# A graph layer's last stage: the output blocks take every fourth node instead of 128 neighbours

## The chip, the cores and the metric

One core of a Trainium2 chip runs the whole kernel in one launch. The metric is the device time in microseconds (us) of one execution. Engines are named as in the profile: PE (TensorE, with PEld for its weight loads), DVE (VectorE), ACT (ScalarE), POOL (GpSimd), SP (SyncE, which here only issues DMAs).

## The reference, cut to what matters

12500 nodes of 128 features, 212500 edges sorted by destination, 8 attention heads of 16. The first part sums messages along the edges into `h`. The change is in what comes after it: a batch norm over all nodes, a residual, and a layer norm over the features of each node.

```python
h = x + h_attn
mean = h.mean(axis=0)
var = jnp.mean((h - mean) ** 2, axis=0)
y = (h - mean) * jax.lax.rsqrt(var + BN_EPS) * bn_gamma + bn_beta
out = _layernorm(x + y, axis=-1)     # (v - mean) / sqrt(var + 1e-5), per node
```

## The kernel before, in words

Most of the time goes to the edges: 208 groups of up to eight tiles of 128 edges, for which rows are gathered, scored and summed into `hx`. `hx` holds `h` transposed, one feature per partition and one node per column. None of that is changed. Near its end the loop is written out by hand (L814 to L878), and batch norm statistics are gathered on the way; `norm_scale` (L407) closes them into a scale `ab[:, 0]` per feature.

The last stage (`last_stage`, L889) then works through the nodes in 25 chunks of 512 columns (`B4`); the last has 212 (`width`, L455). The transposed input `x` lies beside it, loaded as `XR[i]` in the same layout (L464).

For each chunk TensorE makes a PSUM bank `ps` of 128 x 4 x 128: up to 128 nodes on the partitions, four blocks, 128 features. A matmul takes 128 columns of `XR`, `hx` or `Y` as its stationary weights and streams the matrix `cent` (or `scaled_cent`, which carries the batch norm's scale), which subtracts the mean over the features; so the result is turned back to one node per partition and centred at once. Each fp32 matmul appears as two passes in the profile, so four blocks are eight. There are three ways to fill a bank (`centred`, L925):

- Chunks in `AHEAD` (0 to 6, 12, 18) add `x` through `part_of_x` (L746 to L748) and `hx` through L934. For chunks 0 to 6 the part from `x` runs before the statistics are closed (`ahead`, L752).
- Chunks 7, 8 and 9 get scale and residual on VectorE (L908), the rest on GpSimd (L910, L911), into a tile `Y`; L945 then multiplies `Y`.
- L937 or L940 adds the batch norm's shift to those chunks that do not have it.

Then, for each pair of chunks: ScalarE squares the bank and sums, either with one whole square and a reduce on VectorE (L960, L961) or block by block with an accumulator (L965); one root per pair (L967); VectorE takes the reciprocal (L971) and scales the bank into the SBUF tile `o` (L977, L982); a DMA writes `o` to the output (L979, L983). The pairs are (0), (1), (2,3), ... (22,23), (24). The order on the engines is the order of the code (L988 to L998): residual of a pair, centring and variance of the pair two before it, scaling of the pair three before it. Every output DMA is issued from SP, but that of chunk 23 and of chunk 24's partial block from ACT, behind ACT's own work in program order.

In the kernel before, `blocks` (L742) cuts a chunk into runs of 128 neighbouring columns. So partition p of block k holds node 128k + p of the chunk, and a partition's four rows of 512 B lie 64 KB apart in the output. Chunk 24 has a block of 128 and one of 84, and each has a scale and a DMA of its own.

Of the kernel before, what the change touches and what calls it, by code (L numbers as in the profile page):

```python
# [13 lines left out]
OP = mybir.AluOpType  # L14
# [3 lines left out]
P = 128  # L18
# [21 lines left out]
def plan(N, T):  # L40

    n, r = divmod(T - sum(LAST), U)
    sizes = [U] * n + [r] * (r > 0) + list(LAST)
    assert n > 1 and len(sizes) % 2 == 0
    starts = [sum(sizes[:g]) for g in range(len(sizes))]
    cuts = list(range(0, N - 64, CH)) + [N - 64, N]
    due = {}
    thr = [0.0] * len(sizes)
    for j, c in enumerate(cuts[1:]):
        need = (c + (64 if c < N - CH else 24)) * T  # L50
        g = next((g for g, t in enumerate(starts) if t * N >= need), None)
        if g is not None:
            due.setdefault(g, []).append(j)
            thr[g] = float(c)
    return sizes, starts, cuts, due, thr
# [27 lines left out]
def gnn_kernel(  # L83
# [19 lines left out]
    nc = tc.nc  # L103
# [3 lines left out]
    usizes, ustarts, cuts, due, _ = plan(N, T)  # L107
# [39 lines left out]
    hx = consts.tile([P, N + P], F32, name="hx")  # L147
# [47 lines left out]
    cent = consts.tile([P, P], F32, name="cent")  # L195
# [218 lines left out]
    def norm_shift():  # L414
        nc.vector.tensor_mul(ab[:, 1:2], ab[:, 0:1], mv[:, 0:1])
        nc.vector.tensor_sub(ab[:, 1:2], gb[:, 1:2], ab[:, 1:2])
# [33 lines left out]
    B4 = 4 * P  # L450
    NY = -(-N // B4)
    XR = {}
    todo = list(range(NY))

    def width(i):  # L455
        return min(B4, N - i * B4)
# [238 lines left out]
    for q in range(NQ):  # L695
# [3 lines left out]
        for g, a in piece.get(q, []):  # L699
            if a == 0:  # L700
                i = free.pop(0)
# [5 lines left out]
        k = q - first_step  # L707
# [32 lines left out]
    RING = ["ps_e", "ps_e", "ps_q", "ps_q", "ps_t", "ps_t", "ps_a", "ps_m"]  # L740

    def blocks(i):  # L742
        n = width(i)
        return [(k, min(P, n - k * P)) for k in range(-(-n // P))]

    def part_of_x(i, ps):  # L746
        for k, m in blocks(i):
            nc.tensor.matmul(ps[:m, k, :], XR[i][:, k * P:k * P + m], cent, start=(k == 0), stop=False)  # L748

    PX = {}  # L750

    def ahead(i):  # L752
        if i in AHEAD:
            r = RING[i % len(RING)]
            PX[i] = psp.tile([P, 4, P], F32, name=r, bufs=RING.count(r))
            part_of_x(i, PX[i])
# [132 lines left out]
    def last_stage(fin, bank, PX):  # L889
        Y, PY, V = {}, {}, {}  # L890


        pick = fin.tile([P, P], BF16, name="pick", bufs=1)
        nc.gpsimd.memset(pick, 0.0)
        for r in (0, 32, 64):
            nc.gpsimd.memset(pick[r:r + 1], 1.0)
        shift = fin.tile([P, P], BF16, name="shift", bufs=1)
        scaled_cent = fin.tile([P, P], F32, name="scaled_cent", bufs=1)

        def residual(i):  # L900

            c, n = i * B4, width(i)
            if i in AHEAD:
                return
            Y[i] = fin.tile([P, B4], F32, name="y", bufs=8)
            y, h = Y[i][:, :n], hx[:, c:c + n]
            if i in on_vector:
                nc.vector.scalar_tensor_tensor(y, h, ab[:, 0:1], XR[i][:, :n], op0=OP.mult, op1=OP.add)  # L908
            else:
                nc.gpsimd.tensor_scalar(y, h, ab[:, 0:1], ab[:, 1:2], op0=OP.mult, op1=OP.add)  # L910
                nc.gpsimd.tensor_tensor(y, y, XR[i][:, :n], op=OP.add)  # L911

        def split_shift():
            ps = bank(7)[:65, 0, :]
            nc.tensor.matmul(ps, ab[:, 1:2].to_broadcast([P, 65]), cent, start=True, stop=True)
            rest = fin.tile([P, P], F32, name="rest", bufs=1)
            mid = fin.tile([P, P], BF16, name="mid", bufs=1)
            nc.scalar.activation(shift[:65], ps, AF.Copy)
            nc.vector.tensor_sub(rest[:65], ps, shift[:65])
            residual(8)  # L920
            nc.scalar.activation(mid[:65], rest[:65], AF.Copy)
            nc.scalar.activation(shift[32:33], mid[32:33], AF.Copy)
            nc.vector.tensor_sub(shift[64:65], rest[64:65], mid[64:65])

        def centred(i):  # L925
            PY[i] = ps = PX[i] if i in PX else bank(i)
            c, full = i * B4, i in AHEAD
            if i == 0:
                split_shift()
            if full:  # L930
                if i not in PX:
                    part_of_x(i, ps)
                for k, m in blocks(i):
                    nc.tensor.matmul(ps[:m, k, :], hx[:, c + k * P:c + k * P + m], scaled_cent, start=False,  # L934
                                     stop=False)
            if i < 2:
                nc.tensor.matmul(ps, ab[:, 1:2].to_broadcast([P, P]), cent[:, None, :].to_broadcast([P, 4, P]),  # L937
                                 start=False, stop=True)
            elif full or i in on_vector:
                nc.tensor.matmul(ps, pick[:65], shift[:65, None, :].to_broadcast([65, 4, P]), start=not full,  # L940
                                 stop=full)
            if not full:
                whole = i in on_vector
                for k, m in blocks(i):
                    nc.tensor.matmul(ps[:m, k, :], Y[i][:, k * P:k * P + m], cent, start=not whole,  # L945
                                     stop=(k == 3 or not whole))

        def spread(p):
            nb = len(blocks(p[-1]))
            return V[p[0]][:, :len(p), :nb, 0]  # L950

        def variance(p):
            v = fin.tile([P, 2, 4, 1], F32, name="v", bufs=4)
            V[p[0]] = v
            if blocks(p[-1])[-1][1] < P:
                nc.vector.memset(v, 1.0)
            for h, i in sorted(enumerate(p), key=lambda e: e[1] not in by_reduce):
                if i in by_reduce:
                    sq4 = fin.tile([P, 4, P], F32, name="sq4", bufs=2)
                    nc.scalar.activation(sq4, PY[i], AF.Square, scale=P ** -0.5)  # L960
                    nc.vector.tensor_reduce(v[:, h, :, 0], sq4, axis=AX.X, op=OP.add)  # L961
                else:
                    sq = fin.tile([P, P], F32, name="sq")
                    for k, m in blocks(i):
                        nc.scalar.activation(sq[:m], PY[i][:m, k, :], AF.Square, scale=P ** -0.5,  # L965
                                             accum_out=v[:m, h, k, :])
            nc.scalar.activation(spread(p), spread(p), AF.Sqrt, bias=eps)  # L967

        def scaled(p):
            v = V[p[0]]  # L970
            nc.vector.reciprocal(spread(p), spread(p))  # L971
            o = fin.tile([P, 2, 4, P], F32, name="o")
            for h, i in enumerate(p):
                bl = blocks(i)
                c, fb = i * B4, sum(m == P for _, m in bl)
                if fb:
                    nc.vector.tensor_tensor(o[:, h, :fb, :], PY[i][:, :fb, :],  # L977
                                            v[:, h, :fb, :].to_broadcast([P, fb, P]), op=OP.mult)
                    (nc.scalar if i == NY - 2 else nc.sync).dma_start(  # L979
                        out[c:c + fb * P, :].rearrange("(c p) d -> p c d", p=P), o[:, h, :fb, :])  # L980
                for k, m in bl[fb:]:
                    nc.vector.tensor_scalar(o[:m, h, k, :], PY[i][:m, k, :], v[:m, h, k, :], None, op0=OP.mult)  # L982
                    nc.scalar.dma_start(out[c + k * P:c + k * P + m, :], o[:m, h, k, :])  # L983

        nc.vector.tensor_scalar(scaled_cent, cent, ab[:, 0:1], None, op0=OP.mult)
        norm_shift()
        residual(7)
        for i in range(len(pairs) + 5):  # L988
            for f, k in ((residual, i), (centred, i - 2), (variance, i - 2), (scaled, i - 3)):
                if 0 <= k < len(pairs):  # L990
                    if f in (residual, centred):
                        for c in pairs[k]:
                            if c not in Y or f == centred:
                                f(c)
                    else:
                        f(pairs[k])
                    if f == scaled and k == 0:
                        residual(9)  # L998
# [144 lines left out]
```

## Time and profile before

| | |
|---|---|
| three runs | 2698.18, 2701.23 (median), 2709.0 us |
| the profiled execution | 2704.18 us, its span 2702.4 us, 37686 instructions |
| busy share of the span | PE 71%, DVE 61%, POOL 58%, PEld 42%, ACT 24% |
| statistics closed, last stage begins | about 2662 us |
| last matmul pass of the stage ends | 2690.6 us |
| last scale ends, last output DMA issued | 2695.9 us |
| output DMAs | 23 of 256 KB and one of 64 KB from SP, one of 256 KB and one of 42 KB from ACT |

Times inside the execution count from the start of its span. Shares over the whole span say little about this change, since the stage is 40 of 2702 us: it has to be read in stretches and by its own lines. A busy PE in the table means passes in flight, which overlap.

### The profile page before, as it was taken

The numbers are of one execution on the slowest core, as the hardware profiler recorded it, in microseconds if no ns is written. First come the engines' busy times: TensorE is split into PE (matmuls) and PEld (weight loads), VectorE is DVE, ScalarE is ACT, GpSimd is POOL, SyncE is SP. The second block draws the span as 40 slices with busy tenths as digits, with TensorE's granted clock in tenths as the row PEclk, the third lists the DMA queues.
The fourth block names the chain that finished last, engine by engine and source line by source line (L and its number), as shares of the span: only waits on it lengthen the run. The fifth ranks groups of instructions, "written<-read, shape, count | busy, mean of one in ns | idle before, by whom it ended". The sixth has DMA issues, their size and how long they took to land. (4 is left out here: it accounts for less than half of the span.)

```text
span 2702.4 us, 37686 instructions
## 1 busy us (share of the span) xinstructions
PE 1926.2 (71%) x9414; PEld 1144.2 (42%) x9414; DVE 1644.1 (61%) x3598; ACT 658.4 (24%) x2477; POOL 1579.8 (58%) x1673
## 2 busy tenths in 40 slices
PE   7787766767777767667675767667777767677677
PEld 5454433433434434334333444334344434444446
DVE  3456665565666565666554665656656656656577
ACT  2242222222222222222221222222222222222225
POOL 5645665565666666565654666665656665656624
PEclk8888888887888878888777888878778887878899
DMA  7744444444454444454444544444544444544454
GB/s 225 237 138 139 139 133 143 127 145 135 136 144 141 135 140 141 129 151 130 141 139 117 145 134 135 139 140 130 146 134 140 141 141 132 149 133 140 141 174 127
DMA packets 177915, 386.83 MB, mean 143 GB/s; under 512 B 38864, under 2 KB 94713, under 8 KB 177689
## 3 DMA queue, kind: packets, MB, share of 16 engines
q0 software_dynamic: 77552, 210.48, 26.8%
q1 hardware_dynamic: 95972, 171.08, 20.8%
q10 hardware_dynamic: 4163, 2.79, 0.3%
q8 instruction: 77, 1.26, 0.2%
q14 instruction: 151, 1.22, 0.1%
HBM read 364.58 MB, written 19.63 MB: 142 GB/s over the span
## 5 line engine op out<-in xcount | busy, mean ns | idle before, releaser
L225 POOL DMA_INDIRECT slot<-kvd,srcs x1573 | 1491.1, 948 | 1002.3 <-PE ps_m L528 469.5
L547 PE MATMUL ps_e<-ea,w_e 128*128 128x512 f32 x832 | 640.4, 914 | 528.7 <-DMA ea<-eaT 455.1
L560 DVE TENSOR_TENSOR wt<-wt,ps_q 128x512 f32<-128x512 f32 x416 | 267.6, 682 | 501.1 <-PE ps_q L555 153.5
L618 PE MATMUL ps_a<-msg,oh 128*128 128x136 f32 (+1 forms) x3322 | 516.8, 293 | 9.6 <-issue 8.8
L547 PEld LDWEIGHTS ps_e<-ea,w_e 128*128 128x128 f32 x832 | 207.9, 276 | 738.9 <-issue 719.7
L549 ACT ACTIVATE wt<-ps_e 128x512 f32<-128x512 f32 x416 | 243.1, 595 | 1024.9 <-PE ps_e L547 374.9
L618 PEld LDWEIGHTS ps_a<-msg,oh 128*128 128x128 f32 (+1 forms) x3322 | 415.6, 167 | 88.9 <-issue 61.6
L579 DVE TENSOR_TENSOR p<-slot,ps_t 128x512 f32<-128x512 f32 (+1 forms) x408 | 263.3, 671 | 172.0 <-PE ps_e L547 86.0
L568 PE MATMUL ps_t<-ident,wt 128*128 128x128 f32 x1661 | 248.2, 294 | 130.0 <-DVE wt L560 94.5
L568 PEld LDWEIGHTS ps_t<-ident,wt 128*128 128x128 f32 x1661 | 202.1, 150 | 152.4 <-DVE wt L560 107.3
L585 DVE TENSOR_REDUCE s<-p 128x64 f32<-128x1024 f32 (+1 forms) x209 | 251.7, 1204 | 0.2
L594 ACT ACTIVATE ps_m<-s 128x64 f32<-128x64 f32 (+1 forms) x209 | 47.5, 227 | 823.2 <-DVE s L593 468.7
L603 DVE TENSOR_TENSOR msg<-slot,ps_m 128x1024 f32<-128x1024 f32 (+1 forms) x206 | 243.2, 1182 | 0.6 <-ACT ps_m L594 0.6
L555 PE MATMUL ps_q<-ot,q 64*128 64x512 bf16 x1248 | 220.0, 469 | 0.0
L555 PEld LDWEIGHTS <-q 64*128 64x128 bf16 x1248 | 50.6, 106 | 294.0 <-issue 280.3
L508 DVE TENSOR_TENSOR oh<-ps_m,rel_i 128x512 f32<-128x512 f32 x208 | 141.7, 681 | 10.0 <-remote 8.6
L643 PE MATMUL ps_m<-ident,at 128*128 128x128 f32 x412 | 109.9, 352 | 41.4 <-DVE oh L511 22.3
L643 PEld LDWEIGHTS ps_m<-ident,at 128*128 128x128 f32 x412 | 70.1, 214 | 153.5 <-issue 88.6
L579 DVE TENSOR_TENSOR p<-byrow,ps_t 128x128 f32<-128x128 f32 x24 | 6.9, 286 | 157.7 <-DMA byrow<-kvd 118.2
L497 ACT ACTIVATE xw<-hx 128x64 f32 x416 | 84.1, 248 | 62.3 <-issue 58.0
L648 ACT ACTIVATE hx<-ps_m 128x64 f32 x412 | 90.8, 220 | 11.4 <-PE ps_m L644 3.3
L528 PE MATMUL ps_m<-w_q,xw 128*128 128x128 f32 x416 | 82.8, 282 | 10.3 <-issue 8.6
(167 smaller groups left out, 1625.6 us busy)
## 6 DMA issues: line engine op xcount, KB each, us to landing
ea<-eaT SPq DMA_DIRECT2D x207, 512.0 KB
byrow<-kvd SPq DMA_DIRECT2D x3072, 1.0 KB
slot<-kvd,srcs POOLq DMA_INDIRECT x1573
rbq<-relT SPq DMA_DIRECT2D x94, 256.0 KB
kvd<-t SPq DMA_DIRECT2D x24, 512.0 KB
slot<-xT SPq DMA_DIRECT2D x24, 256.0 KB
out<-o SPq DMA_DIRECT2D x23, 256.0 KB
hx<-xT SPq DMA_DIRECT2D x11, 512.0 KB
```

What stands on the lines that cost most here:

```text
L225: return nc.gpsimd.indirect_dma_start(out=out, out_offset=None, in_=table, in_offset=bass.IndirectOffsetOnAxis(ap=srcs[:, e:e + 1], axis=0))
L508: nc.vector.tensor_tensor(one, iota_ps[:, None, :].to_broadcast([P, n, P]), r[:, :n, None].to_broadcast([P, n, P]), op=OP.is_equal)
L547: nc.tensor.matmul(eh, w_e, EA[g][:, a:b, :].rearrange("p a b -> p (a b)"), start=True, stop=True)
L549: nc.scalar.activation(t[:, :(b - a) * P], eh, AF.Copy)
L555: nc.tensor.matmul(QE[g][h], Q3[g][r, k, :], OT[g][r, :(b - a) * P], start=(k == 0), stop=(k == 2))
L560: nc.vector.tensor_tensor(t, t, QE[g][h], op=OP.mult)
L568: nc.tensor.transpose(ps[:, j, :], WT[g][h][:, j * P:(j + 1) * P], ident)
L579: nc.vector.tensor_tensor(PR[g][:, c:d, :], KV[g](c, d, 0), PW[g][i][:, c - a:d - a, :], op=OP.mult)
L585: nc.vector.tensor_reduce(SS[g][:, a:b, :], PR[g][:, a:b, :].rearrange("p t (h d) -> p t h d", d=DH), axis=AX.X, op=OP.add)
L603: nc.vector.tensor_tensor(MSG[g][:, a:b, :P].rearrange("p t (h d) -> p t h d", d=DH), KV[g](a, b, P).rearrange("p t (h d) -> p t h d", d=D ...
L618: nc.tensor.matmul(AGG[g][WN if j >= n else 0:], OH[g][j], MSG[g][:, j, :], start=(j == 0), stop=(j == n - 1))
L643: nc.tensor.matmul(ps, AT[g], ident, start=True, stop=False)
```

## The change

A chunk's four blocks now take every fourth node: block k has the columns k, k + 4, k + 8 and so on. So partition p holds the nodes 4p to 4p + 3 of the chunk, and its four rows are one run of 2 KB in the output. The three matmul lines read their weights with a step of four columns. Chunk 24 (212 nodes) becomes four blocks of 53 instead of one of 128 and one of 84; it has one scale and one DMA. The DMAs of chunks 23 and 24 are issued from ACT.

```diff
     def blocks(i):
-        n = width(i)
-        return [(k, min(P, n - k * P)) for k in range(-(-n // P))]
+        assert width(i) % 4 == 0
+        return [(k, width(i) // 4) for k in range(4)]
 
     def part_of_x(i, ps):
         for k, m in blocks(i):
-            nc.tensor.matmul(ps[:m, k, :], XR[i][:, k * P:k * P + m], cent, start=(k == 0), stop=False)
+            nc.tensor.matmul(ps[:m, k, :], XR[i][:, k:width(i):4], cent, start=(k == 0), stop=False)
...
-                    nc.tensor.matmul(ps[:m, k, :], hx[:, c + k * P:c + k * P + m], scaled_cent, start=False,
+                    nc.tensor.matmul(ps[:m, k, :], hx[:, c + k:c + width(i):4], scaled_cent, start=False,
                                      stop=False)
...
-                    nc.tensor.matmul(ps[:m, k, :], Y[i][:, k * P:k * P + m], cent, start=not whole,
+                    nc.tensor.matmul(ps[:m, k, :], Y[i][:, k:width(i):4], cent, start=not whole,
                                      stop=(k == 3 or not whole))
...
-                bl = blocks(i)
-                c, fb = i * B4, sum(m == P for _, m in bl)
-                if fb:
-                    nc.vector.tensor_tensor(o[:, h, :fb, :], PY[i][:, :fb, :],
-                                            v[:, h, :fb, :].to_broadcast([P, fb, P]), op=OP.mult)
-                    (nc.scalar if i == NY - 2 else nc.sync).dma_start(
-                        out[c:c + fb * P, :].rearrange("(c p) d -> p c d", p=P), o[:, h, :fb, :])
-                for k, m in bl[fb:]:
-                    nc.vector.tensor_scalar(o[:m, h, k, :], PY[i][:m, k, :], v[:m, h, k, :], None, op0=OP.mult)
-                    nc.scalar.dma_start(out[c + k * P:c + k * P + m, :], o[:m, h, k, :])
+                c, n = i * B4, width(i)
+                m = n // 4
+                nc.vector.tensor_tensor(o[:m, h, :, :], PY[i][:m], v[:m, h, :, :].to_broadcast([m, 4, P]), op=OP.mult)
+                (nc.scalar if i >= NY - 2 else nc.sync).dma_start(
+                    out[c:c + n, :].rearrange("(p c) d -> p c d", c=4), o[:m, h, :, :])
```

## The prediction

> **What bounds the kernel now.** The change touches only the last stage, from about 2662 us to the end of a span of 2702.4 us, and seven matmul groups that run ahead of it. I read in this order: the chain of waits there, the timeline of its last ten microseconds, busy time by stretches, the DMA queues, then single lines. The chain first (start, length, engine, tile, line):
>
> ```profile
> 2688.60 0.30 ACT v L967
> ...
> 2691.18 0.49 ACT sq L960
> ...
> 2695.57 0.34 DVE o L982
> ```
>
> From 2670.57 us the chain is ScalarE, two chunks every 2.28 us: one whole square (L960), four block squares (L965, between the lines shown), a root (L967). VectorE scales the last results and the chain stops at L982; behind it only DMA is left. The timeline of the end:
>
> ```profile
> 2693.93 0.28 ACT L965 ACTIVATE sq<-ps_e 128x128 f32<-128x128 f32 x1 [0.48 <-DVE v L971]
> ...
> 2695.29 0.42 ACTq L979 DMA_DIRECT2D out<-o  x1
> ...
> 2695.57 0.34 DVE L982 TENSOR_SCALAR o<-ps_e,v 84x128 f32<-84x128 f32 x1
> 2695.95 1.37 ACTq L983 DMA_DIRECT2D out<-o  x1
> ```
>
> Two stretches (length; busy us and count of PE, PEld, DVE, ACT, POOL; clock; DMA share; GB/s):
>
> ```profile
> 2680.00:2685.00 5.00, 5.00 (x46) 4.98 (x45) 4.51 (x10) 4.75 (x23) 4.83 (x6) 1.00 0.80 223
> ...
> 2699.00:2699.40 0.40, 0.00 (x0) 0.00 (x0) 0.00 (x0) 0.00 (x0) 0.00 (x0) 0.50 0.07 21
> ```
>
> In the steady part TensorE has no idle time, ScalarE hardly any, and DMA is at 80%: three resources are nearly level. In the timeline TensorE's chunk 23 ends at 2689.86 and ScalarE takes it up at 2691.09, so TensorE leads by only 1.2 us. The second row is the very end of the data: a share of 0.07 is one DMA engine of 16, working off what it has left at 21 GB/s. The trace's last packet to out ends at 2699.40; the span ends 3.0 us later.
>
> **What each part costs.**
>
> *PSUM side.* Chunks 0 to 23 keep four blocks of 128 nodes; only which node sits in which partition changes. Matmuls, squares, reduces, roots and scales keep their shapes and waits (laid side by side, the two programs' engine queues differ only at chunk 24). Cost nothing: ScalarE's 2.28 us per pair stays.
>
> *Chunk 24* (212 nodes) goes from blocks of 128 and 84 to four of 53. The two blocks took from 2693.93 to 2694.73 on ScalarE, 0.40 each with the accumulator read. Two more: +0.80, root done at 2695.83. The reciprocal then starts near 2695.98 and the scale at 2696.17. One scale of 512 elements replaces 0.29 and 0.34; L977 shows 0.69 for 512, so it ends at 2696.86, not 2695.91: +0.95, all on the path. Behind the root on ScalarE's queue waits chunk 23's output DMA: its issue slips from 2695.29 to about 2696.1. Its data is then out near 2698.3 (1.45 us from issue to first packet, as before, and eight 2 KB packets per engine), which is not last.
>
> *The output DMAs.* 512 B pieces become 2 KB pieces. Queue rows: the stage (2661 to 2703 us); an SP load of 2 KB pieces (2640.9 to 2645); a store of 120 rows from ACT (2357 to 2358):
>
> ```profile
> q1 hardware_dynamic: 12288, 6.10, 52.2%
> q10 hardware_dynamic: 626, 0.31, 2.7%
> ...
> q1 hardware_dynamic: 576, 1.05, 78.9%
> ...
> q10 hardware_dynamic: 135, 0.03, 14.3%
> ```
>
> Row one: 42 us x 16 engines x 0.522 = 351 us for 11904 data packets and 384 completions, 29 ns per 512 B. Row three: 4.1 x 16 x 0.789 = 52 us for 512 packets, 101 ns per 2 KB (the packet records' median is 84). A chunk so costs a DMA engine 32 x 29 = 0.93 us before and 8 x 84 to 101 = 0.67 to 0.81 after. Chunks come every 1.14 us, so DMA was not the limit; this gain is hidden behind ScalarE, and it only removes the backlog of the slowest engine, the 1 us after 2698.4.
>
> *The last DMA.* Row one splits as 23 x 512 + 128 data packets and 24 x 16 completions; row two as 512 + 84 data and 30 = 16 + 14 completions; row four as 120 + 15. Stores of 3 and 2 rows left 3 and 2. So 128 rows go over 16 engines, 120 over 15, 84 over 14: the largest number up to 16 that divides the rows. **53 is prime: all 53 packets of 2 KB would go to one engine.** The Trainium skill (DMA: Bandwidth & Descriptors, "Why a DMA increments its semaphore by 16 and not by 1") states such a division and puts 127 partitions on one engine; no row here shows a prime above 3.
> One engine needs 53 x 84 ns = 4.45 us by the 2 KB row; 53 x 101 = 5.4 by the loaded mean; 108.5 KB at the lone engine's 21 GB/s = 5.2. I take 4.5: nothing else is then in flight. Issue at 2696.90; first packet 0.9 us later (first store of the stage: issue 2667.15, packet 2668.07) to 1.45 us later (chunk 23's). Data end: 2696.9 + 1.2 + 4.5 = 2702.6 against 2699.40. The 3.0 us behind it stay. **Sum: +3.2 us** (2.8 to 4.3), span 2705.6. The profiled execution took 2704.18, so the like of it would take 2707.4; it lies 3 us over the median of the runs shown (2701.23), and the forecast is given from the median: **2704.4**.
>
> *The weight loads.* Every block's weights (x, hx or y) are now read with a step of four floats, 16 B. The rows that bear on it:
>
> ```profile
> L945 PEld LDWEIGHTS ps_e<-cent,y x36: 153/192/193, 2672.5 to 2690.3; 128*128 128x128 f32 x34, 128*84 128x84 f32 x2
> L937 PEld LDWEIGHTS ps_e<-cent,ab x4: 192/192/192, 2663.1 to 2665.0; 128*128 128x128 f32 x4
> L366 DVE TENSOR_SCALAR keep<-lim,wiota x2: 320/356/392, 45.9 to 46.4; 64x208 f32<-64x208 f32 x2
> L368 DVE TENSOR_SCALAR lim<-lim x1: 377/377/377, 47.1 to 47.1; 128x416 f32<-128x416 f32 x1
> ```
>
> 128 columns take 192 ns, 84 take 153: 0.89 ns a column, 114 ns for 128. The chain has eight passes of a chunk in 0.89 us, 111 ns each. Load and matmul stream are equally long, so a slower load is not hidden: it lengthens every pass. No row shows a stepped weight load. From below: L937 reads with a step of zero and takes the same 192; a gain is excluded, since the moving operand alone sets 111 ns. From above: VectorE reads every second float at L366 (1.7 ns an element, 356/208) against 0.91 at L368: a factor near two. I take no cost, by L937, the nearest row (same instruction, engine and tile size). Also, L940 streams 512 bf16 in 0.22 us on the chain, 0.43 ns an element: an operand can be read twice as often as an fp32 load asks. Both ends stay in the range.
> Against this stands the Trainium skill, Advanced Engine Details and Errata, "SBUF Cachelines": lines are 16 bytes, a line must be hit at least twice for full speed, and a new line at each access is penalised. By that rule, which no row here shows, a step of 16 B would lose on every column, and the time would be that of rival 1.
>
> **Rivals.**
> 1. *TensorE becomes the bound: slower.* If a stepped load takes twice as long, a pass is 0.22 us. For: no slack (stretch above), a lead of 1.2 us, load and stream level. Against: L937, L940. Price: the stage has 27 such groups of 0.89 us (7 + 2 x 2 at L934/L748, 16 at L945): +24.0. The chunks 1 to 3 ahead start at 2648.09 and the next gather waits only until 2651.61: 2.2 late; chunks 4 to 6 add another 2.1. TensorE ends at 2690.6 + 28.3 = 2718.9; behind it chunk 24's 1.6 + 0.3 + 0.35 + 0.69, issue and start 1.2, 4.5, and 3.0: 2730.5, **+28 us**, 2729 by the median. It decides as soon as a pass grows by 5% (1.2 of 24). Halfway (1.5 times) it gives +13, 2714.
> 2. *The last DMA is spread.* If 53 rows went over 14 to 16 engines, data would end at 2696.9 + 1.2 + 4 x 0.1 = 2698.5, **0.9 us faster**. Against: 120 rows used 15.
> 3. *The pieces stay 512 B.* Tile o has its own four-by-128 shape; if runs were not joined, the lone engine needs 212 x 23.5 ns (512 B at 21 to 22 GB/s) = 5.0: **+3.7**. Against: the built program lists the copies as 128x512 and 53x512.
>
> **How the numbers follow.** Forecast (with rival 3, which gives the same time) 0.60; rival 1 in full 0.25, about halfway 0.10; rival 2 0.05. A measurement here can tell about 0.5%, 13.5 us. Slower by more: 0.25 and half of the halfway case, 0.30. Faster by more: nothing left behind the last result is worth 13 us, 0.01. Within: 0.69. The likeliest case alone is 2699 to 2709 (runs before spread 2698 to 2709). The range must reach into rival 1 to leave out under 0.2: 2698 to 2729.
>
> **What would show it.** After: in the stage 3312 packets on the SP queue (23 x 144) and 198 on ACT's (128 + 16 + 53 + 1, the 1 being the lone engine's completion); a DMA share of 0.06 for 4 to 5 us at the end; four squares of 53x128; weight loads at 192 ns and eight passes in 0.89 us. Wrong if L945's loads are longer, TensorE's passes stretch, and ScalarE waits for TensorE between pairs: then it is rival 1. Wrong the other way if the last store shows more than one completion.

## The result and the profile after

Over six runs each, the changed kernel takes 2731.72 us (median), the kernel before 2708.3 us: a ratio of 1.0107, 95% interval 1.0084 to 1.0131. It is slower by 23 to 35 us. The prediction said no change and gave 2704.4; its rival 1 (TensorE becomes the bound, 28 us) is what happened. Ratios compare fast runs alone; one of the ten runs of e1_contig below took 5648.56 us and is not in its ratio.

The profiled execution is the fastest of the six: 2721.36 us, span 2719.5. Its last stage begins 8 us earlier than that of the profiled execution of before. That is no gain of the change: the edge loop lies ahead of it, and the six runs of the kernel before already spread from 2698 to 2713 us. So the stage is best read by itself, from the first matmul of the shift (L915 in both) to the end of the span: 2662.05 to 2702.4 before, 40.4 us; 2653.74 to 2719.5 after, 65.8 us. That is 25.4 us more.

The chain of waits of the changed kernel (start, length, engine, tile, line):

```profile
2648.31 3.73 PE ps_t L748 x16
...
2653.90 0.22 PE ps_m L915 x2
...
2697.83 3.73 PE ps_t L945 x16
2701.56 1.87 PE ps_a L945 x8
2703.43 1.88 PE ps_m L945 x8
...
2705.33 0.61 ACT sq L960
...
2710.32 0.68 DVE o L976
```

ScalarE has left the chain. From 2648 to 2705 us it is TensorE without a gap, and a chunk's eight stepped passes (x8) take 1.74 to 1.88 us, not 0.89. Only the last pair still goes through ScalarE and VectorE. In the kernel before, the last group of TensorE's on the chain and the square behind it were:

```profile
2669.36 0.89 PE ps_t L934 x8
...
2670.57 0.60 ACT sq L960
```

Two lines of weight loads of the changed kernel, min/median/max in ns:

```profile
L945 PEld LDWEIGHTS ps_e<-cent,y x40: 172/329/329, 2671.1 to 2706.0; 128*128 128x128 f32 x32, 128*53 128x53 f32 x8
L937 PEld LDWEIGHTS ps_e<-cent,ab x4: 189/198/208, 2655.7 to 2658.4; 128*128 128x128 f32 x4
```

The loads that the change gave a step went from 192 to 329 ns; L937, whose step is zero as before, went only from 192 to 198. Now the waits of the stage (us in total, times, longest):

```profile
DVE v L961 <- ACT sq L960: 24.1, 12, 3.6
...
ACT sq L960 <- PE ps_q L945: 4.7, 2, 3.3
ACT sq L960 <- PE ps_t L945: 4.7, 2, 3.3
```

ScalarE waits for TensorE's banks, up to 3.3 us at a time, and VectorE waits for ScalarE. Before, the list had two waits of ScalarE's squares for TensorE, 0.5 us each, both before 2671 us. The same in two stretches (length; PE, PEld, DVE, ACT, POOL; clock; DMA share; GB/s):

```profile
2695.00:2700.00 5.00, 5.00 (x23) 4.99 (x23) 1.47 (x4) 2.01 (x10) 0.00 (x0) 1.00 0.28 105
...
2715.00:2716.00 1.00, 0.00 (x0) 0.00 (x0) 0.00 (x0) 0.00 (x0) 0.00 (x0) 0.50 0.06 25
```

TensorE is full with 23 passes in 5 us instead of 46; ScalarE has fallen from 4.75 us of 5 to 2.01, the DMA share from 0.80 to 0.28. The second row is the lone DMA engine, one of 16. The queues of the stage (packets, MB, share) confirm the count:

```profile
q1 hardware_dynamic: 3312, 6.03, 24.7%
q10 hardware_dynamic: 198, 0.37, 1.6%
```

198 on ACT's queue is 128 + 16 for chunk 23 and 53 + 1 for chunk 24: one completion, one engine. The trace has its 53 packets one after the other over 5.57 us.

### The profile page after: what moved, and what is told of

The parts are those of the page before. It is cut to its first block, busy times and chain, and to the rows that moved or that the text cites. A ratio compares the mean times of both kernels' runs of the same rounds, so it can differ in the third digit from the quotient of the medians.

```text
span 2719.5 us, 37695 instructions
## 1 busy us (share of the span) xinstructions
PE 1939.1 (71%) x9418; PEld 1168.1 (43%) x9418; DVE 1642.6 (60%) x3597; ACT 661.5 (24%) x2481; POOL 1581.1 (58%) x1673
## 5 line engine op out<-in xcount | busy, mean ns | idle before, releaser
L547 PE MATMUL ps_e<-ea,w_e 128*128 128x512 f32 x832 | 630.5, 901 | 520.9 <-DMA ea<-eaT 433.9
L618 PE MATMUL ps_a<-msg,oh 128*128 128x136 f32 (+1 forms) x3322 | 515.4, 293 | 9.6 <-issue 9.1
L618 PEld LDWEIGHTS ps_a<-msg,oh 128*128 128x128 f32 (+1 forms) x3322 | 413.9, 166 | 87.2 <-issue 60.1
L555 PEld LDWEIGHTS <-q 64*128 64x128 bf16 x1248 | 50.5, 105 | 290.4 <-issue 276.3
L643 PE MATMUL ps_m<-ident,at 128*128 128x128 f32 x412 | 108.5, 348 | 45.4 <-DVE oh L511 23.2
L643 PEld LDWEIGHTS ps_m<-ident,at 128*128 128x128 f32 x412 | 69.1, 211 | 156.6 <-issue 97.3
```

What stands on the lines that cost most here:

```text
L547: nc.tensor.matmul(eh, w_e, EA[g][:, a:b, :].rearrange("p a b -> p (a b)"), start=True, stop=True)
L555: nc.tensor.matmul(QE[g][h], Q3[g][r, k, :], OT[g][r, :(b - a) * P], start=(k == 0), stop=(k == 2))
L618: nc.tensor.matmul(AGG[g][WN if j >= n else 0:], OH[g][j], MSG[g][:, j, :], start=(j == 0), stop=(j == n - 1))
L643: nc.tensor.matmul(ps, AT[g], ident, start=True, stop=False)
```

## The experiments

**Theory 1.** SBUF serves the weight load by 16 B lines. A load that finds each of its columns in another line is slow; TensorE's passes double, and as TensorE had no slack the stage becomes its sum. The lone DMA engine is a second, small term. **Rivals:** the output DMAs carry the loss (piece size, lone engine); or any step other than one costs the same; or the cost grows with the distance.

The last four kernels ran on another chip, on which the kernel before takes 2122.87 us (median of 13) at a mean granted clock of 0.93, not 0.83. In the stage the granted clock is 1.00 on both, and ratios are to the kernel before on the same chip. "Stage" is the length defined above.

| run | ratio to before, 95% interval | stage, us |
|---|---|---|
| before | 1 | 40.4 |
| the changed kernel | 1.0107 (1.0084 to 1.0131) | 65.8 |
| e1_contig: the change with contiguous weights | 1.0020 (1.0001 to 1.0039) | 43.3 |
| e2_step_only: stepped weights alone | 1.0094 (1.0069 to 1.0118) | 63.0 |
| e4_step2: step of two, runs of 1 KB | 1.0011 (0.9993 to 1.0029) | 40.7 |
| e5_spread: e1 with the last store spread | one run only | 40.6 |
| e6_only_y: 15 of 24 whole chunks by fours | 1.0055 (1.0038 to 1.0072) | 52.9 |
| e7_step3: step of three | 1.0066 (1.0050 to 1.0083) | 51.5 |
| e8_writer_steps: the writer of Y takes the step | 1.0000 (0.9991 to 1.0010) | 40.3 |

**e1_contig: the change without the step.**

```diff
-XR[i][:, k:width(i):4]                # L748; the same at L934 (hx) and L945 (Y)
+XR[i][:, k * m:k * m + m]
```

> The changed kernel with one thing undone: each block's weights are neighbouring columns again (the rows of the output are then in another order). Blocks of a quarter of the chunk, 2 KB pieces and the one DMA of 53 rows stay. Theory 1 (a weight load that finds every column in another 16 B line takes 330 ns, not 192, and TensorE becomes the bound): loads at 192 ns, eight passes in 0.89 us, ScalarE bound again; about 25 us less than the changed kernel, and 2 to 4 us over the kernel before (ratio 1.001), these from the lone DMA engine. Rival (the output DMAs, their size or the lone engine, carry the loss): within 8 us of the changed kernel, ratio 1.008 or more.

Loads are at 192 ns again. The ratio falls to 1.0020, and ScalarE is back on the chain:

```profile
2684.95 0.30 ACT v L967
...
2690.13 0.68 DVE o L976
```

What is left of the loss is 2.9 us of stage. So the step carries nearly all of the 25.4 us, and the DMAs do not.

**e2_step_only: the step without the change.**

```diff
-Y[i][:, k * P:k * P + m]              # the same at L748 and L934
+Y[i][:, k:B4:4]                       # in whole chunks
```

> The kernel before with the stepped weights alone, in the 24 whole chunks (rows then go out in another order); pieces of 512 B, chunk 24 and its DMAs as before. Theory 1: loads at 329 ns, TensorE's last pass about 28 us later after the close of the statistics, ratio 1.009 to 1.010. Rival (the DMAs): ratio under 1.003.

1.0094, and a stage of 63.0 us: +22.6. With the 2.9 of e1 that makes 25.5, against 25.4 for the whole change. From the close of the statistics (L416 in both) TensorE's last pass comes 25.6 us later than before, a little less than the 28 expected. Its chain ends as that of the changed kernel, in TensorE's passes at twice their length, and then as that of before:

```profile
2713.14 1.88 PE ps_m L948 x8
...
2719.55 0.34 DVE o L985
```

**e3_steps: one step per chunk.** One run, with each step on a line of its own.

```diff
-w = hx[:, c + k * P:c + k * P + m]
+w = hx[:, c + k:c + k + 127 * s + 1:s]   # s = 1, 2, 3, 4, 5, 8, 16, 2 in chunks 0 to 6, 18
+matmul(ps[:m, k, :], scaled_cent, hx[:, c + k:c + B4:4], ...)   # chunk 12
```

> The kernel before; only the weights from hx at the residual matmul of chunks 0, 1, 2, 3, 4, 5, 6, 18 are read with a step of 1, 2, 3, 4, 5, 8, 16, 2 floats, and in chunk 12 it is the moving operand that is read from hx with a step of 4 (these chunks' values are then others). Theory 1 (lines of 16 B, two hits needed): 192 ns at steps 1 and 2, something between at 3 (four columns in three lines), 329 at 4, 5, 8 and 16 alike. Rival A (any step but one costs the same): 329 from step 2 on. Rival B (cost grows with the distance): 2 a little over 192, 8 and 16 well over 329. For the moving operand: by theory 1 its pass grows too, from 0.11 to 0.22 us; if only the load's path is slow, it stays.

Steps 1, 2, 3, 4 and 8, and the moving operand of chunk 12 (min/median/max ns):

```profile
L938 PEld LDWEIGHTS ps_e<-scaled_cent,hx x8: 186/192/192, 2667.8 to 2668.6; 128*128 128x128 f32 x8
L940 PEld LDWEIGHTS ps_e<-scaled_cent,hx x8: 196/198/199, 2669.3 to 2670.4; 128*128 128x128 f32 x8
L942 PEld LDWEIGHTS ps_q<-scaled_cent,hx x8: 251/262/264, 2671.1 to 2672.5; 128*128 128x128 f32 x8
L944 PEld LDWEIGHTS ps_q<-scaled_cent,hx x8: 309/330/330, 2672.8 to 2674.4; 128*128 128x128 f32 x8
L948 PEld LDWEIGHTS ps_t<-scaled_cent,hx x8: 314/336/338, 2676.7 to 2678.3; 128*128 128x128 f32 x8
L952 PE MATMUL ps_t<-hx,scaled_cent x8: 386/407/409, 2686.8 to 2688.4; 128*128 128x128 f32 x8
```

Step 2 costs 6 ns, step 3 costs 70, step 4 costs 138, and beyond that it does not rise: 314 at step 5, 336 at 8, 311 at 16. Both rivals on the step fall: the cost is not the same for every step but one, and it does not grow with the distance beyond 16 B. A load's record also moves a little with what runs beside it (the contiguous loads of chunk 12 took 208 ns), so the groups of eight passes in the chain are the better measure: 0.94 us at step 2, 1.33 at 3, 1.75 at 4 and 1.80 at 8, against 0.89 for contiguous weights. The moving operand pays too: 407 instead of 275 ns, 1.82 us per eight. Why steps 5 and 16 are some 6% cheaper than 4 and 8 stays open.

**e4_step2: as much of the idea as is nearly free.**

```diff
+s = c + k // 2 * 2 * P + k % 2
-Y[i][:, k * P:k * P + m]              # the same at L748 and L934
+Y[i][:, s:s + 2 * P - 1:2]            # s from c = 0 here and at L748
-out[c:c + fb * P, :].rearrange("(c p) d -> p c d", p=P)
+out[c:c + B4, :].rearrange("(b p c) d -> p b (c d)", b=2, c=2)
```

> The kernel before with a step of two: blocks 0 and 1 take the even and odd nodes of the first 256 of a chunk, 2 and 3 those of the second, so that each partition writes two runs of 1 KB; chunk 24 as before. Theory 1: loads at 192 ns, no cost; the DMA gain stays hidden behind ScalarE, ratio 1.000 within 0.002 (at best 1 us from the backlog of the slowest DMA engine). Rival A: loads at 329 ns, ratio 1.009 to 1.010.

Loads at 196 ns, ratio 1.0011 with 1 inside the interval: in the total the step of two costs nothing that can be measured, and runs of 1 KB bring nothing either. TensorE does pay for it, and the chain shows it:

```profile
2678.85 1.88 PE ps_q L949 x16
...
2683.81 0.60 ACT sq L964
```

Two groups take 1.88 us, so one takes 0.94, 5% more than 0.89. With that TensorE holds the chain for 18 us of the stage, until 2683.81; in the kernel before ScalarE takes over after 8.5 us. The stage is still only 0.3 us longer; with a step of three (e7) it is 11 us longer.

**e5_spread: the second term.**

```diff
-dma_start(to, o[:53, h, :, :])            # ACT
+dma_start(to[:48], o[:48, h, :, :])       # ACT
+dma_start(to[48:53], o[48:53, h, :, :])   # SP
```

> As the run with contiguous weights (rows in another order), but chunk 24's store of 53 rows is cut in 48 rows from ACT and 5 from SP. Theory 1 with the lone engine as the second, small term: 16 and 5 completions instead of one; from the issue of the store to the last packet about 2 us, not 7; the stage, from the first matmul of the shift to the end of the span, 39 to 40 us, against 43.3 with the store of 53 rows and 40.4 in the kernel before. If the lone engine is not the cause of the 2.9 us: 43 us again.

The queues of its stage:

```profile
q1 hardware_dynamic: 3322, 6.04, 38.1%
q10 hardware_dynamic: 208, 0.36, 2.6%
```

208 is 128 + 16 + 48 + 16, and 3322 is the 3312 of the changed kernel and 5 + 5: 16 and 5 engines. The last packet ends 2.4 us after the last issue, and the stage is 40.6 us (39 to 40 expected), not 43.3. By these two traces, which come from two chips, the lone engine cost 2.7 us.

**e6_only_y: the price per group.**

```diff
+fours = width(i) == B4 and i not in AHEAD
-Y[i][:, k * P:k * P + m]
+Y[i][:, k:B4:4]                           # if fours, and the store "(p c) d -> p c d" with it
```

> The kernel before, with every fourth node, stepped weights and 2 KB pieces only in the 15 whole chunks that go through Y; the nine chunks ahead and chunk 24 as before. Theory 1, with a price per group of eight passes of 0.86 us and a lead of about 1 us to use up: stage longer by 15 x 0.86 - 1 = 12 us (from 40.4 to 52), ratio 1.0045. If the loss hangs on the chunks ahead, or is a single event: under 3 us, or over 20.

52.9 us against 52 expected, ratio 1.0055. (The ratio expected, 1.0045, is 12 us of 2700; of this chip's 2123 us they are 1.0057.) The loss grows with the number of stepped groups, as the sum of a bound engine does. Its waits show ScalarE behind TensorE:

```profile
ACT sq L963 <- PE ps_m L948: 3.3, 3, 1.3
ACT sq L963 <- PE ps_e L948: 2.9, 2, 1.6
```

**e7_step3: the price per line.**

```diff
-Y[i][:, k * P:k * P + m]              # the same at L748 and L934
+Y[i][:, k:k + 3 * P - 2:3]            # in whole chunks
```

> The kernel before with a weight step of three floats in all whole chunks (columns then overlap and the values are others). Theory 1 with a price per line touched: loads at 262 ns, groups of eight at 1.33 us, 26 groups x 0.43 - 1 = 10 us in the stage (50.5 us), 1 to 2 more ahead of it, ratio 1.004. If TensorE only binds beyond a larger slack: stage under 44 us.

A stage of 51.5 us (50.5 expected) and a ratio of 1.0066. The 1.004 expected was again for 2700 us; 1.0066 is 14 us, of which 11.1 lie in the stage. The prediction's halfway case had priced passes of 1.5 times the length at 13 us. Three groups of the chain:

```profile
2115.19 1.33 PE ps_q L948 x8
...
2119.32 1.40 PE ps_a L948 x8
2120.72 1.42 PE ps_m L948 x8
```

Half the slowdown of a pass gives half the loss of e2 (11.1 of 22.6 us): TensorE has hardly any slack that would hide it.

Groups right behind a matmul of the shift are shorter (1.33 here, 1.75 at step 4). Those that follow another group directly give the price of a line: 1.40 us for eight passes at step 3, 1.87 at step 4 (the changed kernel) and 0.94 at step 2 (e4). The 128 columns of a pass lie in 96, 128 and 64 lines of 16 B, which makes 1.82, 1.83 and 1.84 ns a line. One price fits all three. Contiguous columns lie in 32 lines, 59 ns at that price. That is less than the 111 ns that a pass takes anyway, so there the price does not show.

**e8_writer_steps: the step on another engine.**

```diff
+q = lambda a: a.rearrange("p (q k) -> p q k", k=4)
-nc.gpsimd.tensor_tensor(y, y, XR[i][:, :n], op=OP.add)
+nc.gpsimd.tensor_tensor(y.rearrange("p (k q) -> p q k", k=4), q(t), q(XR[i][:, :n]), op=OP.add)
```

VectorE's line for chunks 7 to 9 likewise; the store as in e6.

> The kernel before, with every fourth node and 2 KB pieces in the 15 whole chunks that go through Y, but the weights contiguous: GpSimd (and VectorE for chunks 7 to 9) writes Y in block order, 512 B from one element to the next. Theory 1: TensorE's loads stay at 192 ns, and the time is that of the writers. If a stepped write costs them nothing: stage 40 to 41 us, ratio 1.000. If it costs GpSimd half as much again on 1.27 us (12 writes): stage 47 to 49, ratio 1.003.

The writers' lines in the stage (busy us, mean ns):

```profile
L922 POOL TENSOR_TENSOR y<-yt,slot 128x512 f32<-128x512 f32 x12 | 16.0, 1329 | 1.0
```

```profile
L912 DVE SCALAR_TENSOR_TENSOR y<-hx,ab,slot 128x512 f32<-128x512 f32 x3 | 3.6, 1194 | 0.0
```

GpSimd writes with a step of 512 B in 1329 ns against 1299. VectorE's three writes, early in the stage, take 1.11, 1.35 and 1.12 us against 0.74 in the kernel before. That is not all the step's doing: in e7, where this line writes contiguously, the second and third took 1.27 and 1.60 us while GpSimd worked beside it. The first took 0.74 to 0.75 us in every run but e8, so there the step most likely costs about 0.37 us. Part of VectorE's loss lies on the chain, but the stage is no longer for it: 40.3 us. Ratio 1.0000 (0.9991 to 1.0010): runs of 2 KB in 15 chunks at no loss, and no gain. No version tried beats the kernel before; the list of its waits in the stage has none for an output DMA.

## Why the prediction was wrong, step by step

- *What bounds the stage.* Right: ScalarE with TensorE 1.2 us ahead of it, three resources nearly level, so that a slower pass would show at once. e6 and e7 confirm it, and so does e4, where passes 5% longer, the prediction's tipping point, put TensorE on the chain for 18 us.
- *PSUM side at no cost.* Right: e1 has ScalarE's pace unchanged.
- *Chunk 24.* Right: from the first of its four squares to the root took 1.58 us (1.6 expected), the scale 0.68.
- *The output DMAs.* Right that the gain is hidden (e4, e8).
- *The last DMA on one engine, +3.2 with chunk 24's two squares.* Right in kind and size: 2.9 us of stage in e1, all but 0.2 gone in e5. In the changed kernel the 53 packets took 5.57 us, not 4.5: 47 took 84 to 87 ns as assumed, but six took 141 to 498. What held those six up no run shows.
- *The weight loads.* **This step failed: "I take no cost, by L937, the nearest row".** L937 reads one element again and again, so it stays in one line; as a row for a step of four it says nothing, however near its instruction is. L940 misled in the same way: it reads twice as many elements in a time, but eight bf16 to a line, 64 lines in 0.22 us or 3.4 ns a line. A step of four asks for a line every 0.87 ns and gets one every 1.8. None of the prediction's TensorE rows asked for lines faster than one in 3.4 ns, so the rows left the question open, and the sum should not have been closed at their lower end. What the runs showed in place of "no cost": loads of 329 ns for 192, groups of 1.87 us for 0.89, TensorE as the bound, and 22.6 us of stage by the step alone (e2). The Trainium skill's rule (Advanced Engine Details and Errata, "SBUF Cachelines": two hits on a line of 16 bytes for full speed) was on the table as the case against. The runs agree with it but for a small rest: a load took 198 ns at two hits a line, 262 at 1.33 and 330 at one, where contiguous weights took 192, and at two hits a pass was still 5% longer (e4).
- *The upper end, a factor of two from VectorE's L366.* Right in size by luck. L366 has a step of two floats, and at that step TensorE's loads cost only 3% more. What makes L366 slow on VectorE no run here shows.
- *Rival 1's price.* Right: +28 worked out; 25.4 in the stage, and ahead of it 2.3 from chunks 4 to 6 (the last sum's matmul at L643 to L915 takes 6.15 us, 3.88 before) and 2.5 from chunks 1 to 3 (from their first L748 to the next gather's L618 is 6.04 us, 3.56 before), about 30 in all, against 29 by the ratio. Its chance, 0.25, was held down by L937 and L940, which said nothing against it, and the upper end of the range, 2729, lay at the rival's own time, so the range cut through it. Of the 27.3 us between 2704.4 and 2731.72, 7.1 have nothing to do with the change: the kernel before ran that much slower in the six runs than in the three shown.

## What to carry to other kernels

Ask of every stepped operand how many 16 B lines it touches per column, and how long its engine has for one: here a line cost TensorE 1.8 ns, so a pass with fp32 weights at a step of two floats took 5% longer and one at a step of four took twice as long. A layout that makes DMA runs longer pays only where the profile shows someone waiting for the DMA; if it is wanted anyway, put the step on a writer with slack (e8) or stop at a step of two (e4). And count a store's rows: here 53, a prime above 16, went out through a single DMA engine, while 48 went through 16 and 5 through 5.

## What the runs showed that was not expected

- A stepped *moving* operand, of which the prediction had said nothing, pays as well: 407 ns for 275 at a step of four (e3).
- Writing with a step of 512 B cost GpSimd about 2% (1329 for 1299 ns) for 512 floats, and VectorE about half as much again (1.11 for 0.74 us, in the first of its three writes) (e8). The same line of VectorE, written contiguously, took up to 1.60 us in e7, so part of e8's longer times may not be the step's.
- Two chips took 2703 and 2123 us (medians) for the same kernel, with mean granted clocks of 0.83 and 0.93. The clocks differ by 12%, the times by 27%; no run shows where the rest comes from. The last stage has a granted clock of 1.00 on both. There is no trace of the kernel before from the second chip, but e8 and e5 there, at 40.3 and 40.6 us, are close to its 40.4 on the first.
